# Hyperbolic loops of a graph kernel: two row blocks at once in halves of TensorE, the 65th coordinate apart, a degree-3 polynomial, tiles of 2x512

## The chip, the cores and the metric

The kernel runs on one core of a Trainium2 chip. The metric is the time of one execution on the device, in microseconds (us). An engine is named as the profile names it: PE is TensorE (PEld its weight loads), ACT is ScalarE, DVE is VectorE, POOL is GpSimd, SP is SyncE.

## The reference

Four graph layers follow each other on 3327 nodes of 64 features. Each takes `h = relu(layernorm(x))` and adds its result to `x`. Layers 0 and 3 are hyperbolic and are what is changed here; layers 1 and 2 (a decayed sum over neighbours, and a signed attention with two GRU cells) stay as they are. A hyperbolic layer, with c = 1 for layer 0 and c = 1/r^2 for layer 3:

```python
x_tan = _logmap0(x, C)
left = x_tan @ att_W[:D] + att_b
right = x_tan @ att_W[D:]
adj_att = jax.nn.sigmoid(left + right.T) * adj
x_local = _logmap(x[:, None, :], x[None, :, :], C)
support_t = jnp.einsum('ij,ijd->id', adj_att, x_local)
return _proj(_expmap(x, support_t, C), C)
```

`_logmap` of a pair of nodes needs their scalar product and their squared lengths, then an artanh. So for every pair of the 3327 x 3327 there is a product of two vectors, a function of it, a sigmoid and a mask, and the results are summed over neighbours with the vectors as weights. `adj` holds zeros and ones; about 0.5% are ones.

## The kernel before

The nodes are padded to 3328 = 26 blocks of 128 (T = 26, P = 128, NP = 3328, D = 64). `adj` comes in transposed, so that the neighbours lie on the partitions. The program first runs `hyperbolic_series` (layer 0, `adj` read from memory), `plain_decay` (which also builds masks of 8 bits), `plain_gat`, and `hyperbolic_series` again (layer 3, with the masks), and stores the result. Each part also writes whether its shortcuts held for all nodes; if one did not, a second, general path computes everything anew. In `hyperbolic_series` that test is `x2 >= X2_MIN`, the squared length of every real node.

`hyperbolic_series` has three stages.

1. Preparation. `norm_relu` makes H (node on the partition). `rows` holds per node 65 numbers: 64 coordinates 2*h/(x2-1) and as the 65th (x2+1)/(x2-1). `to_columns` (L114, L115: transposes on PE, copies on ACT) turns `rows` into LT, 65 x 3328; RT is LT with the first 64 rows negated, so that a product of LT and RT over 65 rows gives the argument of the polynomial for a pair. The tangent vectors `xt` are transposed too (`xtT`). `pl` (L333) multiplies them with the left half of the weights, spread over 128 columns, which makes `leftB`, the left term on every partition; `pr` (L337) makes `right`, one column per block.
2. The loop. It goes over four column chunks of 832 nodes and in each over 13 pairs of row blocks. For a pair: the mask (13 DMAs per chunk in the first call, masks in the second; `drop_diagonal`, L146, clears the diagonal), two sigmoids on ACT (L357), one product with the mask on POOL (L359). Then for each of the two row blocks: two matmuls of 416 columns into L (L364), two Square passes on ACT that make a polynomial of degree 4 (L368, L369), two combined operations on DVE (L370, L372), which give the weights w, and two matmuls that add `rows` x w into `acc` (L375), 65 x 416 each. L has three buffers, y and w two, `acc` one. All data of these matmuls are f32.
3. The end. `acc` is copied (L379), turned back by `to_rows` (L124), scaled (L389), and `move` does the remaining steps on DVE for all nodes at once.

The program is written with a framework that sets the waits and orders each engine's instructions by a planned order of its own; on PE, products of later blocks stand ahead of sums of earlier ones.

In `plain_decay` and `plain_gat`, matmuls with 64 weight columns stand in pairs that write the two halves of the partitions of one accumulator (L909, L974), with 16-bit weights and 16- or 8-bit data:

```python
for o in range(2):
    PE.matmul(acc[h][o * D:(o + 1) * D, :], parts[k][:, b, :], w[:, o, h, :],
              start=first and k == 0, stop=last and k == 2)
```

Of the kernel before, what the change touches and what calls it, by code (L numbers as in the profile page):

```python
# [9 lines left out]
F32 = mybir.dt.float32  # L10
# [8 lines left out]
P = 128  # L19
# [9 lines left out]
G0, G1, G2, G3, G4 = 0.30970640316, -0.36098355479, 0.46940675477, -1.28660460234, 2.86920527402  # L29
X2_MIN = 18.0  # L30
# [3 lines left out]
def tile_gnn4(ctx: ExitStack, tc: tile.TileContext, x, adjT, att0, b0, w1, bias1, w_gat, a_gat,  # L34
# [26 lines left out]
    g1_c = column(G1 - 0.5, "g1_c")  # L61
    g2_c = column(G2, "g2_c")
# [8 lines left out]
    def wide(t, n=D):  # L71

        return t[:, :, None].to_broadcast([P, T, n])
# [161 lines left out]
    def hyperbolic_series(att, b_att, r, min_norm, min_norm2, ok, masks=None):  # L235
# [8 lines left out]
        W = 2 * BK  # L244
        R = D + 1
        with ExitStack() as st:
            pers = st.enter_context(tc.tile_pool(name="hs", bufs=1))
            rows = pers.tile([P, T, R], F32, name="rows")
# [3 lines left out]
            LT = pers.tile([R, NP], F32, name="LT")  # L252
            RT = pers.tile([R, NP], F32, name="RT")
            leftB = pers.tile([P, NP], F32, name="leftB")
            right = pers.tile([P, T], F32, name="right")
            maxn2 = pers.tile([P, 1], F32, name="maxn2")
# [3 lines left out]
            with tc.tile_pool(name="hsp", bufs=1) as tp, tc.tile_pool(name="hsps", bufs=2, space=PSUM) as ps:  # L260
                w_l = tp.tile([D, 1], F32, name="w_l")
                w_r = tp.tile([D, 1], F32, name="w_r")
                nc.sync.dma_start(w_l, att[:D])
                nc.sync.dma_start(w_r, att[D:])
                bcol = tp.tile([P, 1], F32, name="bcol")
                nc.scalar.dma_start(bcol, bcast_rows(b_att))
                w_lb = tp.tile([D, P], F32, name="w_lb")
                V.tensor_copy(w_lb, w_l.to_broadcast([D, P]))
# [30 lines left out]
                V.tensor_mul(rows[:, :, :D], hs, wide(ia))  # L299
                V.tensor_scalar(rows[:, :, :D], rows[:, :, :D], 2.0, None, op0=OP.mult)  # L300
                V.scalar_tensor_tensor(rows[:, :, D], x2, 1.0, ia, op0=OP.add, op1=OP.mult)
# [19 lines left out]
                xt = tp.tile([P, T, D], F32, name="ln_sq")  # L321
                V.tensor_mul(xt, H, wide(z))

                to_columns(ps, LT, rows, R)
                sgn = tp.tile([R, 1], F32, name="sgn")
                V.memset(sgn, 1.0)
                V.memset(sgn[:D], -1.0)
                V.tensor_scalar(RT, LT, sgn, None, op0=OP.mult)
                xtT = tp.tile([D, NP], F32, name="xtT")
                to_columns(ps, xtT, xt, D)  # L330
                for k in range(NP // BK):
                    pl = ps.tile([P, BK], F32, name="pl")
                    PE.matmul(pl, w_lb, xtT[:, k * BK:(k + 1) * BK], start=True, stop=True)  # L333
                    V.tensor_copy(leftB[:, k * BK:(k + 1) * BK], pl)
                pr = ps.tile([P, T], F32, name="pr")
                for t in range(T):
                    PE.matmul(pr[:, t:t + 1], xtT[:, t * P:(t + 1) * P], w_r, start=True, stop=True)  # L337
                V.tensor_scalar(right, pr, bcol, None, op0=OP.add)  # L338

            with tc.tile_pool(name="hsw", bufs=2) as wk, tc.tile_pool(name="hsps", bufs=3, space=PSUM) as ps, \  # L340
                    tc.tile_pool(name="hsacc", bufs=1, space=PSUM) as pa:
                for c in range(NP // W):
                    c0 = c * W
                    acc = [pa.tile([R, BK], F32, name=f"acc{h}") for h in range(2)]
                    for b2 in range(T // 2):
                        if masks is None:
                            adj = wk.tile([P, 2, W], F32, name="adj", bufs=4)
                            nc.sync.dma_start(adj, adjT[2 * b2 * P:(2 * b2 + 2) * P, c0:c0 + W]
                                              .rearrange("(s p) i -> p s i", p=P))
                            for s in range(2):  # L350
                                drop_diagonal(adj[:, s, :], 2 * b2 + s, c0, W)
                        else:
                            adj = masks[b2][:, :, c0:c0 + W]
                        sig = wk.tile([P, 2, W], F32, name="sig")
                        for s in range(2):
                            b = 2 * b2 + s
                            A.activation(sig[:, s, :], leftB[:, c0:c0 + W], AF.Sigmoid,  # L357
                                         bias=right[:, b:b + 1])
                        G.tensor_tensor(sig, adj, sig, op=OP.mult)  # L359
                        for s in range(2):  # L360
                            b = 2 * b2 + s
                            L = ps.tile([P, 2, 512], F32, name="L")
                            for h in range(2):
                                PE.matmul(L[:, h, :BK], LT[:, b * P:(b + 1) * P],  # L364
                                          RT[:, c0 + h * BK:c0 + (h + 1) * BK], start=True, stop=True)
                            Lu = L[:, :, :BK]
                            y = wk.tile([P, 2, BK], F32, name="y")
                            A.activation(y, Lu, AF.Square, scale=0.5, bias=g1_c)  # L368
                            A.activation(y, y, AF.Square, bias=g2_c)  # L369
                            V.scalar_tensor_tensor(Lu, Lu, 0.5 * G3, y, op0=OP.mult, op1=OP.add)  # L370
# [729 lines left out]
```

## Time and profile before

| what | value |
|---|---|
| time, median of 3 runs (lowest, highest) | 1271.29 us (1270.71, 1277.21) |
| the profiled execution: its own time, its span | 1277.46 us, 1275.7 us |
| mean granted TensorE clock in it | 0.895 |
| busy: PE, DVE, ACT, POOL | 997.5, 823.7, 726.2, 393.6 us |
| loop of the first hyperbolic call, start to its last sums | 57.7 to 395.2 us |
| loop of the second hyperbolic call | 889.6 to 1216.5 us |

The profile is one execution, and the times in it are counted from the start of its span. A group of instructions is one line of the kernel on one engine with one kind of operands: its count, its busy time, the mean length of one, then the idle time of the engine just before them and what ended most of it. A record of a matmul is longer than the spacing of matmuls, because they are pipelined: what one costs in a row of many is read from the distance of their starts, and in the timeline from a merged group (its length less that of the last record, divided by the count less one). The first words of a group's operands give weights and output partitions: 128*64 is 128 rows by 64 columns of weights.

### The profile page before, as it was taken

The page shows a single profiled execution, that of the slowest core. Times are in us where ns is not written, and L with a number is a line of the kernel's source. Part 1 is how long each engine was busy: PE and PEld are TensorE (multiplying, and loading weights), DVE is VectorE, ACT ScalarE, POOL GpSimd, SP SyncE. Part 2 cuts the span into 40 slices and gives each one's busy share as a digit, 9 for nine tenths or more (in the row PEclk, how much of TensorE's full clock was granted, in tenths as well). Part 3 has the DMA queues.
Part 4 walks back from the last instruction along what each step waited for, and adds up shares of the span by engine and source line. Part 5 has one row for each costly group of instructions (what it writes and reads, how often), then busy time and mean ns, then how long its engine had stood idle before and what let it go on. Part 6 is the DMA issues. An engine that isn't in the chain of part 4 may idle for free.

```text
span 1275.7 us, 11381 instructions
## 1 busy us (share of the span) xinstructions
PE 997.5 (78%) x4051; PEld 477.7 (37%) x4051; DVE 823.7 (65%) x937; ACT 726.2 (57%) x851; POOL 393.6 (31%) x166
## 2 busy tenths in 40 slices
PE   0989999999993037888996699919899998999910
PEld 0634444344441032333332476406344443444400
DVE  7255666566668969994933402793466676667787
ACT  1378879889883013444453001413689999899910
POOL 0065665665661000201210000000445555455500
PEclk9789989999997568999999799966799999999965
DMA  2153444444420009992910000000000000000001
GB/s 28 57 171 121 134 134 134 134 136 135 139 101 0 0 21 341 302 305 82 297 47 9 6 2 1 1 0 1 0 1 1 0 1 1 0 1 1 0 3 28
DMA packets 41844, 91.62 MB, mean 72 GB/s; under 512 B 15152, under 2 KB 15152, under 8 KB 41776
## 3 DMA queue, kind: packets, MB, share of 16 engines
q1 hardware_dynamic: 37200, 90.76, 21.9%
q10 hardware_dynamic: 4576, 0.02, 0.3%
q8 instruction: 34, 0.56, 0.2%
q14 instruction: 34, 0.28, 0.1%
HBM read 89.92 MB, written 0.85 MB: 71 GB/s over the span
## 4 chain that ended last, share of the span: by engine, by line
PE 45%; DVE 22%; ACT 17%; POOL 7%; issue 6%; DMA 2%; ACTq 0%; DVEq 0%; POOLq 0%; SPq 0%
PE acc L375 13%; PE L L364 9%; POOL sig L359 7%; PE acc L909 6%; ACT y L369 5%; DVE w L372 5%; PE acc L974 4%; ACT w L902 4%; PE cnt L904 4%; ACT sig L357 3%; ACT y L368 3%; DVE L L370 3%; PE cnt L900 2%; PE pt L114 2%; DVE prod L153 1%
## 5 line engine op out<-in xcount | busy, mean ns | idle before, releaser
L375 PE MATMUL acc<-w,rows 128*65 128x416 f32 x832 | 341.3, 535 | 39.9 <-DVE w L372 38.1
L364 PE MATMUL L<-RT,LT 65*128 65x416 f32 x832 | 334.2, 527 | 0.7 <-DVE right L338 0.7
L370 DVE SCALAR_TENSOR_TENSOR L<-L,y 128x832 f32<-128x832 f32 x208 | 213.8, 1030 | 185.4 <-ACT y L369 181.7
L359 POOL TENSOR_TENSOR sig<-mask,sig 128x1664 f32<-128x1664 fp8e4 x52 | 164.6, 3167 | 385.2 <-ACT sig L357 375.1
L372 DVE SCALAR_TENSOR_TENSOR w<-L,sig 128x832 f32<-128x832 f32 x208 | 212.5, 1024 | 52.9 <-POOL sig L359 35.8
L368 ACT ACTIVATE y<-L,g_c 128x832 f32<-128x832 f32 x208 | 195.8, 943 | 76.5 <-PE L L364 76.5
L359 POOL TENSOR_TENSOR sig<-adj,sig 128x1664 f32<-128x1664 f32 x52 | 193.1, 3716 | 102.2 <-ACT sig L357 102.1
L364 PEld LDWEIGHTS L<-RT,LT 65*128 65x128 f32 x832 | 162.6, 196 | 149.9 <-issue 146.9
L369 ACT ACTIVATE y<-y,g_c 128x832 f32<-128x832 f32 x208 | 203.9, 983 | 3.5
L357 ACT ACTIVATE sig<-leftB,right 128x832 f32<-128x832 f32 x208 | 201.2, 977 | 7.5 <-DVE w L372 7.4
L375 PEld LDWEIGHTS acc<-w,rows 128*65 128x65 f32 x832 | 108.9, 141 | 242.7 <-DVE w L372 117.1
L902 ACT ACTIVATE w<-cnt,ebias 128x832 bf16<-128x832 f32 x104 | 93.7, 950 | 110.9 <-PE cnt L900 68.8
L146 POOL TENSOR_TENSOR mask<-mask,offdiag 128x128 fp8e4<-128x128 fp8e4 x26 | 23.4, 902 | 248.0 <-PE cnt L904 241.6
L895 DVE SCALAR_TENSOR_TENSOR same<-adj 128x1664 bf16<-128x1664 f32 x52 | 99.0, 1904 | 0.0
L909 PE MATMUL acc<-w,sup 128*64 128x416 bf16 x624 | 94.0, 349 | 0.0
L904 PE MATMUL cnt<-mask,rest 128*128 128x416 fp8e4 x208 | 54.1, 341 | 28.7 <-ACT w L902 28.7
L900 PE MATMUL cnt<-mask,after 128*128 128x416 fp8e4 x208 | 55.2, 350 | 9.7 <-DVE mask L892 9.7
L974 PE MATMUL acc<-mask,h 128*64 128x416 fp8e4 x624 | 60.9, 345 | 0.7 <-ACT hP L827 0.7
L909 PEld LDWEIGHTS <-sup 128*64 128x64 bf16 x624 | 38.1, 110 | 49.9 <-issue 37.0
L892 DVE TENSOR_SCALAR mask<-adj 128x1664 fp8e4<-128x1664 f32 x52 | 54.9, 1056 | 1.1 <-DMA adj<-in 1.1
L114 PE MATMUL pt<-ident,rows 128*65 128x128 f32 x52 | 12.0, 426 | 54.4 <-DVE zs L86 30.2
L114 PE MATMUL pt<-ident,H 128*64 128x128 f32 x26 | 5.3, 366 | 61.4 <-DVE H L106 61.4
(247 smaller groups left out, 657.9 us busy)
## 6 DMA issues: line engine op xcount, KB each, us to landing
adj<-in SPq DMA_DIRECT2D x104, 832.0 KB, 4.8
X<-in SPq DMA_DIRECT2D x1, 832.0 KB, 7.8
out<-X SPq DMA_DIRECT2D x1, 832.0 KB, 6.0
gw<-in SPq DMA_DIRECT2D x8, 48.0 KB, 2.3
gb<-in ACTq DMA_DIRECT2D x8, 0.8 KB, 2.0
w_l<-in SPq DMA_DIRECT2D x2, 0.2 KB, 5.2
bcol<-in ACTq DMA_DIRECT2D x2, 0.5 KB, 5.4
w_r<-in SPq DMA_DIRECT2D x2, 0.2 KB, 4.1
```

The source lines that it names most:

```text
L357: A.activation(sig[:, s, :], leftB[:, c0:c0 + W], AF.Sigmoid, bias=right[:, b:b + 1])
L359: G.tensor_tensor(sig, adj, sig, op=OP.mult)
L364: PE.matmul(L[:, h, :BK], LT[:, b * P:(b + 1) * P], RT[:, c0 + h * BK:c0 + (h + 1) * BK], start=True, stop=True)
L368: A.activation(y, Lu, AF.Square, scale=0.5, bias=g1_c)
L369: A.activation(y, y, AF.Square, bias=g2_c)
L370: V.scalar_tensor_tensor(Lu, Lu, 0.5 * G3, y, op0=OP.mult, op1=OP.add)
L372: V.scalar_tensor_tensor(w, Lu, G4 - 0.5 * G3, sig[:, s, :].rearrange("p (h i) -> p h i", h=2), op0=OP.add, op1=OP.mult)
L375: PE.matmul(acc[h], rows[:, b, :], w[:, h, :], start=(b == 0), stop=(b == T - 1))
L902: A.activation(w[:, o, :, :], cnt[o][:, :, :BK], AF.Exp, scale=-LN2, bias=ebias)
L904: PE.matmul(cnt[o][:, h, :BK], rest, mask[:, o, h * BK:(h + 1) * BK], start=False, stop=True, skip_group_check=True)
L909: PE.matmul(acc[h][o * D:(o + 1) * D, :], parts[k][:, b, :], w[:, o, h, :], start=first and k == 0, stop=last and k == 2)
L974: PE.matmul((acc[k] if i < 3 else cnt[k])[o * D:(o + 1) * D, :], w, mask[:, o * HP + k * BK:o * HP + (k + 1) * BK], start=b == 0 and i in ...
```

## The change

The loops of both hyperbolic calls get another form, and what they need is prepared and finished otherwise.

- *Products.* The 64 coordinates are laid out twice, on partitions 0 to 63 and 64 to 127 (XT). The products of two row blocks use rows 0 to 63 and 64 to 127 of the array (L415). The 65th coordinate is split into three 16-bit parts; its product, with a constant added, is a matmul of 9 rows in 16 bits per row block, on rows 0 to 31 and 32 to 63 (E and F, transposed into ET and FT; L419).
- *Polynomial.* Degree 3 instead of 4: one Square on ACT per tile instead of two (L422), a combined operation and a product on DVE (L423, L425). The threshold X2_MIN goes from 18 to 22.
- *Tiles.* One tile holds both row blocks by 512 columns; there are seven column chunks, six of 512 and one of 256. y, L and w are handled once per pair of row blocks.
- *Sums.* The sums of the two row blocks go into the two halves of one accumulator (L428), and those of the 65th coordinate into one of four groups of 32 columns of a second one (L433; `rows0` holds the coordinate and 31 zeros). At the end of a chunk both are copied by ACT (L438) and folded and transposed by matmuls with `halves` and `one_c` (L444, L445) into M.
- *Left and right.* They are made by DVE (a product and a sum over the features each) instead of by matmuls; `left` is put as three 16-bit parts into F and spread over the partitions at the start of each chunk by a matmul with `pick` (L394).

All line numbers in this section are those of the changed kernel. The diff, cut to its core:

```diff
-G0, G1, G2, G3, G4 = 0.30970640316, -0.36098355479, 0.46940675477, -1.28660460234, 2.86920527402
-X2_MIN = 18.0
+G0, G1, G2, G3 = -0.3851200397, -1.4315723663, 0.0289761757, 1.8129648238
+X2_MIN = 22.0
...
-        W = 2 * BK
-        R = D + 1
+        W = 512
+        NF = 12
...
+                for t0 in range(0, T, 4):
+                    n = min(4, T - t0)
+                    pt = ps.tile([P, 4 * P], F32, name="pt")
+                    for k in range(n):
+                        PE.transpose(pt[:D, k * P:(k + 1) * P], rows[:, t0 + k, :], ident)
+                        PE.matmul(pt[D:, k * P:(k + 1) * P], rows[:, t0 + k, :], ident, start=True, stop=True)
+                    A.activation(XT[:, t0 * P:(t0 + n) * P], pt[:, :n * P], AF.Copy)
...
-                xt = tp.tile([P, T, D], F32, name="ln_sq")
-                V.tensor_mul(xt, H, wide(z))
-
-                to_columns(ps, LT, rows, R)
...
-                to_columns(ps, xtT, xt, D)
-                for k in range(NP // BK):
-                    pl = ps.tile([P, BK], F32, name="pl")
-                    PE.matmul(pl, w_lb, xtT[:, k * BK:(k + 1) * BK], start=True, stop=True)
-                    V.tensor_copy(leftB[:, k * BK:(k + 1) * BK], pl)
-                pr = ps.tile([P, T], F32, name="pr")
-                for t in range(T):
-                    PE.matmul(pr[:, t:t + 1], xtT[:, t * P:(t + 1) * P], w_r, start=True, stop=True)
+                for k, o in ((0, left), (1, right)):
+                    sq = tp.tile([P, T, D], F32, name="ln_sq")
+                    V.tensor_mul(sq, H, wlr[:, k, None, :].to_broadcast([P, T, D]))
+                    V.reduce_sum(o, sq, axis=AX.X)
+                    V.tensor_mul(o, o, z)
...
+                pl = parts3(left, "pl")
+                V.tensor_copy(F[:, :, 9:12], pl)
+                for dst, src in ((ET, E), (FT, F)):
+                    to_columns(ps, dst, src, D)
...
+                    PE.matmul(Ll[:, 0, :n], pick, FT[:NF, cs], start=True, stop=True)
+                    leftB = wk.tile([P, W], F32, name="leftB", bufs=2)
+                    V.tensor_copy(leftB[:, :n], Ll[:, 0, :n])
...
-                            for h in range(2):
-                                PE.matmul(L[:, h, :BK], LT[:, b * P:(b + 1) * P],
-                                          RT[:, c0 + h * BK:c0 + (h + 1) * BK], start=True, stop=True)
...
-                            A.activation(y, Lu, AF.Square, scale=0.5, bias=g1_c)
-                            A.activation(y, y, AF.Square, bias=g2_c)
-                            V.scalar_tensor_tensor(Lu, Lu, 0.5 * G3, y, op0=OP.mult, op1=OP.add)
...
-                            for h in range(2):
-                                PE.matmul(acc[h], rows[:, b, :], w[:, h, :],
-                                          start=(b == 0), stop=(b == T - 1))
+                        for s in range(2):
+                            q, e = slice(s * D, (s + 1) * D), slice(s * 32, s * 32 + 9)
+                            b = slice((2 * b2 + s) * P, (2 * b2 + s + 1) * P)
+                            PE.matmul(L[:, s, :], XT[q, b], XT[q, cs], start=True, stop=False)
+                        for s in range(2):
+                            q, e = slice(s * D, (s + 1) * D), slice(s * 32, s * 32 + 9)
+                            b = slice((2 * b2 + s) * P, (2 * b2 + s + 1) * P)
+                            PE.matmul(L[:, s, :], ET[e, b], FT[e, cs], start=False, stop=True)
+
+                        y = wk.tile([P, 2, W], F32, name="y", bufs=2)[:, :, :n]
+                        A.activation(y, L, AF.Square, scale=-0.5, bias=shift_c)
+                        V.scalar_tensor_tensor(L, y, G3, L, op0=OP.add, op1=OP.mult)
+                        w = wk.tile([P, 2, W], F32, name="w")[:, :, :n]
+                        V.tensor_mul(w, L, sig)
                         for s in range(2):
                             b = 2 * b2 + s
+                            PE.matmul(accs[0][s * D:(s + 1) * D, :n], rows[:, b, :], w[:, s, :],
+                                      start=b2 == 0, stop=b2 == T // 2 - 1)
...
+                            g = b % 4 * 32
+                            PE.matmul(accs[1][g:g + 32, :n], rows0[:, b, :], w[:, s, :],
+                                      start=b < 4, stop=b >= T - 4)
...
+                    for k in range(nt):
+                        PE.matmul(Lm[:, k, :D], sums[0][:, k * P:(k + 1) * P], halves, start=True, stop=True)
+                        PE.matmul(Lm[:, k, D:], sums[1][:, k * P:(k + 1) * P], one_c, start=True, stop=True)
+                    V.tensor_copy(M[:, t0:t0 + nt, :], Lm)
...
-                to_rows(ps, RT, R, lambda t0, n, src: V.tensor_copy(M[:, t0:t0 + n, :], src))
```

## The prediction

> **What bounds the kernel now.** I read the page first (busy shares, slices, the chain that ended last, groups), then the busy time in the two stretches where the changed loops run, then the timeline for starts. From the page:
>
> ```profile
> PE 997.5 (78%) x4051; PEld 477.7 (37%) x4051; DVE 823.7 (65%) x937; ACT 726.2 (57%) x851; POOL 393.6 (31%) x166
> PE 45%; DVE 22%; ACT 17%; POOL 7%; issue 6%; DMA 2%; ACTq 0%; DVEq 0%; POOLq 0%; SPq 0%
> L375 PE MATMUL acc<-w,rows 128*65 128x416 f32 x832 | 341.3, 535 | 39.9 <-DVE w L372 38.1
> L364 PE MATMUL L<-RT,LT 65*128 65x416 f32 x832 | 334.2, 527 | 0.7 <-DVE right L338 0.7
> L370 DVE SCALAR_TENSOR_TENSOR L<-L,y 128x832 f32<-128x832 f32 x208 | 213.8, 1030 | 185.4 <-ACT y L369 181.7
> L368 ACT ACTIVATE y<-L,g_c 128x832 f32<-128x832 f32 x208 | 195.8, 943 | 76.5 <-PE L L364 76.5
> L357 ACT ACTIVATE sig<-leftB,right 128x832 f32<-128x832 f32 x208 | 201.2, 977 | 7.5 <-DVE w L372 7.4
> ```
>
> TensorE leads the chain, and L364 and L375 have 832 records each where the program issues 416 calls: an f32 matmul is two records, each with a weight load of its own. The two loops, first call and second (columns: stretch, length, busy time of PE, PEld, DVE, ACT, POOL, then the granted clock):
>
> ```profile
> 57.70:395.20 337.50, 314.51 (x833) 136.51 (x834) 210.91 (x208) 285.39 (x320) 204.40 (x80) 0.96 0.41 132
> 889.60:1216.50 326.90, 310.02 (x833) 135.31 (x834) 212.26 (x208) 284.65 (x320) 164.62 (x52) 0.96 0.00 1
> ```
>
> PE is busy 93 to 95%, ACT 85%: so the price of a matmul sets these 664.4 us. The timeline gives prices by starts (start, length of the group):
>
> ```profile
> 1100.38 1.56 PE L364 MATMUL L<-RT,LT 65*128 65x416 f32 x4
> ...
> 730.54 2.29 PE L974 MATMUL acc<-mask,h 128*64 128x416 fp8e4 x24
> ...
> 541.80 0.52 PE L904 MATMUL cnt<-mask,rest 128*128 128x416 fp8e4 x2
> 542.25 1.24 PE L909 MATMUL acc<-w,sup 128*64 128x416 bf16 x10
> 543.42 0.35 PE L900 MATMUL cnt<-mask,after 128*128 128x416 fp8e4 x1
> ...
> 38.30 0.96 PE L333 MATMUL pl<-xtT,w_lb 64*128 64x416 f32 x2
> ...
> 43.36 0.94 PE L337 MATMUL pr<-w_r,xtT 64*128 64x1 f32 x8
> ```
>
> - f32: (1.56 - 0.51 of the last record) / 3 = 0.35 us per record of 416 columns. A loop has 832: 291 us, of 337.5 and 326.9. The rest is some 10 us of halved clock and the waits.
> - Halves of columns do overlap in 16 and 8 bits: L974 alternates between the halves and needs (2.29 - 0.34) / 23 = 0.085 us per record, half of a full-width record (two of L904: 0.52 - 0.34 = 0.18).
> - Going from full width to halves costs: L904's last stream ends at 541.80 + 2 x 0.175 = 542.15, L909 starts at 542.25; back again its last pair ends near 542.25 + 1.24 - 0.34 + 0.175 = 543.33 and L900 starts at 543.42. Some 0.095 us each way.
> - After a switch the weight load is exposed too: L333, first after transposes in another form, starts its second record 0.96 - 0.51 = 0.45 us after the first, 0.10 over the usual 0.35.
> - A matmul of one column with 128 f32 weights (L337) costs (0.94 - 0.25) / 7 = 0.10 us, 0.11 without the first start, which overlaps.
>
> **The change, part by part.** The unit is now a pair of row blocks by 512 columns: 6 x 13 = 78 full pairs and 13 half-wide ones per loop. In units of such area the old loop paid 337.5/84.5 = 3.99 and 326.9/84.5 = 3.87 us.
>
> *Other engines.* By slopes between 416 (0.60, 0.65 us) and 832 columns, ACT pays 2 x 0.69 + 1.12 = 2.5 us a pair (before 2.90 x 1024/832 = 3.6; the second Square is gone), DVE 1.21 + 1.20 = 2.4 as before, POOL 3.72 x 1024/1664 = 2.3. All lie under PE, so the shorter polynomial and the wider tile buy only fewer waits.
>
> *TensorE.* One f32 record of 512 columns streams 0.35 x 512/416 = 0.43 us, one bf16 record 0.175 x 512/416 = 0.215. A pair needs X (two products of 64 rows, f32), E (two of 9 rows, bf16), A (two sums into 64 columns, f32), C (two sums into 32 columns, f32); every one is in another form of the array than its neighbour, so a pair has four switches: 0.095 each plus the exposed load, X 0.20, E 0.11, A 0.145, C 0.12, together 0.575.
>
> How far X, A and C overlap is the open cost; no row shows an f32 matmul in halves, or halves of rows in any type. Each issues first block high, first block low, second block high, second block low. The low record needs the half that the high one is streaming into. In all stretches that I read matmuls start in the program's order: none overtakes an earlier one. So the second block can't start with the first block's high record, only with its low one: three slots instead of four (L974 alternates at every record, and so gets two at once). I take that, since it follows from L974's overlap and the order of starts alike; the ends are two slots (as L974) and four (no overlap). With three: X 1.29 + 0.20, E 0.215 + 0.11, A 1.29 + 0.145, C 1.29 + 0.12 = 4.66 us; half-wide 2.62. Per loop 78 x 4.66 + 13 x 2.62 = 397.5.
>
> The order in which the program issues TensorE's work adds to it: of 182 X pairs 48, or 24 per loop, are split by A and C of another pair, each at one slot and one switch more: 24 x 0.63 = 15. New are the closing sums (L444, L445: 26 blocks x 4 records x 0.11 = 11.5) and the spreading of `left` (7 x 0.33 = 2.3, switches 1.4). Sum 428; halved clock 10 as before; at each of seven column ends PE waits for the copies of the sums, some 0.7 (a 512-wide ACT copy) + 0.3: 7. So 445 per loop. The next chunk's chain (left copied, sigmoid, mask, w: about 6 us) hides behind three pairs of X and E and the closing sums, 3 x 1.8 + 2 us; without that cover 3 us per chunk. Over both loops 2 x 445 - 664.4 = +226.
>
> A rule speaks against the change twice. The Trainium skill, "TensorEngine Tiling (Array Packing)", Key Properties, says that a change of tiling mode, not of tile, drains the engine; the rows above agree at 0.095 us. The Trainium skill, "TensorE: Matmul & The Clock Gate", Part 3, says that matmuls are strictly first in, first out in start and end, while its span model has packed tiles 4 ns apart; by the first the sum is that above, by the second alone each f32 pair would take two slots, the rival below.
>
> *Before and after the loops.* Gone are `pl` (8 matmuls), `pr` (26) and the transposes of `xt`:
>
> ```profile
> 46.90 2.98 PE pl L333 x4
> 49.88 7.49 PE pr L337 x36
> ```
>
> In come 52 transposes for E and F, of which F's 26 wait for the last of `left`: 52 records of 0.11 to 0.21 us (full or halved clock), about what `pr` cost. DVE gains two products and two reductions (7.5 us) and some 30 small operations (3 to 6), loses 4.9; PE loses pl's 16 records (6 to 11). Net -4 a call, then -1.5 for the row transposes at the end: -11 in all, between -25 and +5. `leftB` by chunk puts a copy before the first sigmoid (+1, in that).
>
> Sum against the profiled execution (1277.46 us, span 1275.7): 1277.5 + 226 - 11 = 1492; the median of the runs lies 6 lower: **1486 us**.
>
> **The rivals.**
> - *Full overlap, switches as measured.* If the second block starts with the first: X 1.06, E 0.325, A 1.005, C 0.98 = 3.37 a pair; the loop 263 + 26 (half-wide) + 24 x 1.06 for the split ones + 15 + 17 = 346: 1277.5 + 27 - 11 - 6 = 1288, up to 1340 if PE still waits for w as it does now. The four switches eat what the halves save. For it: L974's pairs. Against: the order of starts.
> - *Full overlap and free switches: faster.* If the next form's weights load while the last one streams, each pair saves 0.575 more, 57 per loop: 1288 - 114 = 1174. It needs both; the sign turns when the switches of a pair cost under about 0.47 us. Against: the 0.095 and 0.10 us above; for: those rows are from other types and forms, and a switch between two forms of halves is not among them.
> - *Columns overlap, rows don't* (no row shows the latter): X +0.43, E +0.215: +44 per loop, 1574.
> - *No overlap in f32 at all:* 6.16 a pair, loop 562: 1720.
> - That the second path runs (nodes under the new threshold 22): worked out from the reference's inputs, the smallest is 23.5, so no.
>
> **How the numbers follow.** Three slots 0.50; columns only 0.08; no overlap 0.05; full overlap at measured switches 0.17 (0.04 of it within half a per cent, about what a measurement of this kernel can tell from no change); full overlap with cheap switches 0.20. Slower 0.50 + 0.08 + 0.05 + 0.13 = 0.76, same 0.04, faster 0.20. The range reaches to the columns-only case with its error, 1600, leaving out the last, and down to 1225, leaving out about half of the fast case (1174 to 1265). The likeliest case's own range is 1430 to 1530 (exposed loads 0.3 to 0.8 a pair).
>
> **What would show it.** In the profile after: starts of L415 and L428 in an X or A group at 0, 0.43, 0.43, 0.86 us (three slots) against 0, 0, 0.43, 0.43; a gap of 0.1 us or more at each change among L415, L419, L428, L433; PE busy over 95% in the loops with ACT and DVE under 60%; loops of 430 to 460 us. Wrong if the second block's first record starts with the first block's, if starts after a switch come without a gap, or if a loop's rest is idle time before PE.

## The result, and the profile after

The changed kernel takes **1369.22 us** (median of 4 runs, 1366.99 to 1372.89). The kernel before, on the same chip, takes 1272.87 us. The ratio is 1.0755, 95% interval 1.0716 to 1.0794. It is slower, as forecast, by 96 us where 215 was forecast (1486 less the 1271.29 of before); the time lies between the rival "full overlap, switches as measured" (1288, up to 1340) and the forecast of 1486.

The page's lines that answer to those of before (line, engine, operands, count; busy time, mean length; idle time before, and what ended it):

```profile
PE 1068.5 (78%) x5125; PEld 374.1 (27%) x5125; DVE 835.9 (61%) x961; ACT 584.9 (43%) x799; POOL 416.6 (30%) x254
...
PE 22%; DVE 9%; ACT 3%; issue 1%; DVEq 0%; ACTq 0%
...
L423 DVE SCALAR_TENSOR_TENSOR L<-y,L 128x1024 f32<-128x1024 f32 (+1 forms) x182 | 209.7, 1152 | 220.7 <-ACT y L422 220.7
...
L415 PE MATMUL L<-XT 64*128 64x512 f32 (+1 forms) x728 | 258.0, 648 | 0.0
...
L428 PE MATMUL acc<-w,rows 128*64 128x512 f32 (+1 forms) x728 | 190.3, 602 | 52.6 <-DVE w L425 52.6
...
L433 PE MATMUL acc<-w,rows 128*32 128x512 f32 (+1 forms) x728 | 184.4, 586 | 0.0
```

ACT has fallen from 726 to 585 us and DVE has stayed, as forecast; PE has grown, and the sums L428 wait 52.6 us for w. The chain that ended last accounts for only 35% of this span, so its shares are not compared with those of before. The busy time in the two loops of the changed kernel (stretch, length, busy PE, PEld, DVE, ACT, POOL, granted clock):

```profile
67.27:432.20 364.93, 337.53 (x1379) 88.16 (x1378) 215.87 (x195) 210.70 (x288) 210.66 (x117) 0.97 0.42 122
939.06:1309.40 370.34, 345.15 (x1379) 89.06 (x1378) 215.97 (x195) 210.88 (x288) 171.43 (x91) 0.95 0.00 1
```

The loops hold 735.3 us in place of 664.4: +71. The first starts at 67.3 instead of 57.7 us, 506.9 us lie between them instead of 494.4, and the tail is 1.6 us shorter: +20.5 outside the loops, where -11 was forecast.

The timeline of PE in the first loop shows what a pair costs (start, length of the group, form, records):

```profile
201.35 1.13 PE L415 MATMUL L<-XT 64*128 64x512 f32 x4
202.41 1.08 PE L428 MATMUL acc<-w,rows 128*64 128x512 f32 x4
203.42 1.05 PE L433 MATMUL acc<-w,rows 128*32 128x512 f32 x4
204.40 0.39 PE L419 MATMUL L<-FT,ET 9*128 9x512 bf16 x2
205.28 1.08 PE L428 MATMUL acc<-w,rows 128*64 128x512 f32 x4 [0.49 <-DVE w L425]
206.29 1.05 PE L433 MATMUL acc<-w,rows 128*32 128x512 f32 x4
207.27 1.13 PE L415 MATMUL L<-XT 64*128 64x512 f32 x4
208.34 0.39 PE L419 MATMUL L<-FT,ET 9*128 9x512 bf16 x2
208.65 1.13 PE L415 MATMUL L<-XT 64*128 64x512 f32 x4
```

Four records of X, A or C occupy two slots, not three: A starts 202.41 - 201.35 = 1.06 us after X, C 1.01 after A, E 0.98 after C, and X 0.31 after E. That sums to 3.36 us a pair; the rival said 3.37, the forecast 4.66. In the trace's records the first two X start at 201.349 and 201.355, the next two at 201.882 and 201.888. Two pairs repeat every 7.30 us (201.35 to 208.65): 6.73 of work, and 0.56 that the sums wait for w.

Not all products have this rhythm. In each loop 48 groups of X hold the two records of one product alone, with other work before and behind them (start, length of the group, form, records):

```profile
181.53 1.12 PE L415 MATMUL L<-XT 64*128 64x512 f32 x2
182.58 0.39 PE L419 MATMUL L<-FT,ET 9*128 9x512 bf16 x2
182.90 1.13 PE L415 MATMUL L<-XT 64*128 64x512 f32 x4
183.96 0.39 PE L419 MATMUL L<-FT,ET 9*128 9x512 bf16 x2
```

Such a group takes 182.58 - 181.53 = 1.05 us, as long as four records of two blocks (183.96 - 182.90 = 1.06). Against 24 groups of four with the same records, 48 groups of two cost some 25 us more per loop.

### The profile page after: what moved, and what is told of

It is laid out like the page before. It is cut to its first block, busy times and chain, and to the rows that moved or that the text cites. A ratio compares the mean times of both kernels' runs of the same rounds, so it can differ in the third digit from the quotient of the medians.

```text
span 1367.1 us, 13434 instructions
## 1 busy us (share of the span) xinstructions
PE 1068.5 (78%) x5125; PEld 374.1 (27%) x5125; DVE 835.9 (61%) x961; ACT 584.9 (43%) x799; POOL 416.6 (30%) x254
## 5 line engine op out<-in xcount | busy, mean ns | idle before, releaser
L423 DVE SCALAR_TENSOR_TENSOR L<-y,L 128x1024 f32<-128x1024 f32 (+1 forms) x182 | 209.7, 1152 | 220.7 <-ACT y L422 220.7
L422 ACT ACTIVATE y<-L,shift_c 128x1024 f32<-128x1024 f32 (+1 forms) x182 | 190.9, 1049 | 179.3 <-PE L L419 179.3
L408 ACT ACTIVATE sig<-leftB,right 128x512 f32<-128x512 f32 (+1 forms) x364 | 233.7, 682 | 77.6 <-DVE w L425 67.9
L415 PE MATMUL L<-XT 64*128 64x512 f32 (+1 forms) x728 | 258.0, 648 | 0.0
L410 POOL TENSOR_TENSOR sig<-mask,sig 128x1024 f32<-128x1024 fp8e4 (+1 forms) x91 | 171.4, 1887 | 250.6 <-ACT sig L408 202.3
L410 POOL TENSOR_TENSOR sig<-adj,sig 128x1024 f32<-128x1024 f32 (+1 forms) x91 | 199.7, 2202 | 139.9 <-ACT sig L408 111.9
L428 PE MATMUL acc<-w,rows 128*64 128x512 f32 (+1 forms) x728 | 190.3, 602 | 52.6 <-DVE w L425 52.6
L425 DVE TENSOR_TENSOR w<-L,sig 128x1024 f32<-128x1024 f32 (+1 forms) x182 | 209.1, 1149 | 21.5 <-POOL sig L410 2.0
L433 PE MATMUL acc<-w,rows 128*32 128x512 f32 (+1 forms) x728 | 184.4, 586 | 0.0
L415 PEld LDWEIGHTS L<-XT 64*128 64x128 f32 x728 | 71.8, 194 | 102.4 <-issue 95.8
L428 PEld LDWEIGHTS acc<-w,rows 128*64 128x64 f32 x728 | 36.5, 137 | 157.8 <-DVE w L425 130.8
L419 PE MATMUL L<-FT,ET 9*128 9x512 bf16 (+1 forms) x364 | 70.3, 383 | 0.0
L343 PE MATMUL pt<-ident,rows 128*64 128x128 f32 x52 | 21.9, 421 | 59.6 <-DVE rows L336 31.1
L433 PEld LDWEIGHTS acc<-w,rows 128*32 128x32 f32 x728 | 26.5, 109 | 141.0 <-issue 141.0
```

The source lines that it names most:

```text
L408: A.activation(sig[:, s, :], leftB[:, :n], AF.Sigmoid, bias=right[:, 2 * b2 + s:2 * b2 + s + 1])
L415: PE.matmul(L[:, s, :], XT[q, b], XT[q, cs], start=True, stop=False)
L419: PE.matmul(L[:, s, :], ET[e, b], FT[e, cs], start=False, stop=True)
L422: A.activation(y, L, AF.Square, scale=-0.5, bias=shift_c)
L423: V.scalar_tensor_tensor(L, y, G3, L, op0=OP.add, op1=OP.mult)
L425: V.tensor_mul(w, L, sig)
```

## The experiments

Theory: the halves overlap in full, switches of form cost what the prediction read, and the rest of the loss is the waits for w, the preparation and the clock. Rivals: the loss is partial overlap; the loss is the switches alone; the loss belongs to the polynomial or the wide tile. Beside each run stood runs of the kernel before on the same chip (medians 1271.7 to 1274.5 us), and the ratios are to these. How long the clock was halved is read from the clock records of the trace; the granted clock in the rows is their mean.

**Both products in the same half.**

```diff
-PE.matmul(L[:, s, :], XT[q, b], XT[q, cs], start=True, stop=False)
+PE.matmul(L[:, s, :], XT[:D, b], XT[:D, cs], start=True, stop=False)
```

> The changed kernel, but both products of a pair use rows 0 to 63 of the array (the result stays the same, since both halves hold the same data). Theory (the two halves really run at once: in the trace after, records of the two halves start 0.007 us apart and the next two 0.43 to 0.53 later): the products then take four streams of 0.43 us instead of two, +0.86 us a full pair, of which the 0.29 us that PE now waits per pair for w may absorb a part; over 2 x 84.5 pairs +96 to +145 us, so 1465 to 1515 us. Rival (three streams, as predicted before: only one of the four records overlaps): +0.43 us less the wait, +24 to +73 us. Rival (starts are shown together, but the streams share one path): no change, 1369.

Measured: 1549.71 us, ratio 1.2186 (1.2142 to 1.2230); loops 457 and 454. From PE's timeline in this kernel:

```profile
219.71 1.98 PE L415 MATMUL L<-XT 64*128 64x512 f32 x4
221.62 0.39 PE L419 MATMUL L<-FT,ET 9*128 9x512 bf16 x2
221.94 1.98 PE L415 MATMUL L<-XT 64*128 64x512 f32 x4
```

The four X now take 221.62 - 219.71 = 1.91 us, four streams of 0.43 and the switch, where they took 1.06. So two blocks overlap because they lie in different halves, and all of the overlap is there in the changed kernel. The total is 35 us over the upper bound; in this run the clock is halved for 143 and 138 us of the loops (20.5 and 37.5 in the changed kernel), which was not in the estimate.

**Two of the four switches taken away**: E in 64 rows (the same form as X), C in 64 columns (the same form as A).

```diff
-rows0 = pers.tile([P, T, 32], F32, name="rows0")
+rows0 = pers.tile([P, T, D], F32, name="rows0")
...
-PE.matmul(L[:, s, :], ET[e, b], FT[e, cs], start=False, stop=True)
+PE.matmul(L[:, s, :], ET[q, b], FT[q, cs], start=False, stop=True)
...
-PE.matmul(accs[1][g:g + 32, :n], rows0[:, b, :], w[:, s, :], ...)
+PE.matmul(accs[1][s * D:(s + 1) * D, :n], rows0[:, b, :], w[:, s, :], ...)
```

> The changed kernel, with two of the four switches of form of a pair taken away and nothing else: E has 64 rows (zeros below the 9) like X, C has 64 columns (one full, 63 zeros) like A. Theory (each of these two switches costs the 0.10 us that the trace after shows between forms, and the cycle E, y, L, w, A, C, X, E sets a period of 7.3 us for two pairs, in which two of the switches lie): -0.1 us a pair, 1345 to 1360 us. Rival (PE's work alone decides): -0.2 us a pair, 1325 to 1340. Rival (what stands between forms is not the change of form but the load of other weights): no change, 1369.

Measured: 1354.92 us, ratio 1.0642 (1.0587 to 1.0698); loops 357.4 and 359.9. A and C (now L432) in PE's timeline of this kernel:

```profile
204.64 1.08 PE L428 MATMUL acc<-w,rows 128*64 128x512 f32 x4
205.55 1.03 PE L432 MATMUL acc<-w,rows 128*64 128x512 f32 x4
```

and its line among the waits (who waits for whom: us in total, times, the longest):

```profile
PE acc L428 <- DVE w L425: 71.8, 71, 4.3
```

From A to C it is now 0.91 us instead of 1.01: the last A record's stream goes from 0.52 to 0.42 us before the next form begins. A switch costs PE 0.10 us, as read from the kernel before. But the wait for w grew from 52.6 to 71.8 us, and two switches gave 14 us in all. Of the 7.5 and 10.4 us by which the loops fell, some 7 in the second are less halved clock (23.9 us in place of 37.5). That the loop was limited in part by the chain E, y, L, w, which fewer switches don't shorten, is argued from the longer wait.

**XT by one transpose of doubled rows.**

```diff
-for k in range(n):
-    PE.transpose(pt[:D, k * P:(k + 1) * P], rows[:, t0 + k, :], ident)
-    PE.matmul(pt[D:, k * P:(k + 1) * P], rows[:, t0 + k, :], ident, start=True, stop=True)
-A.activation(XT[:, t0 * P:(t0 + n) * P], pt[:, :n * P], AF.Copy)
...
+V.tensor_copy(rows2, rows[:, :, None, :].to_broadcast([P, T, 2, D]))
+to_columns(ps, XT, rows2.rearrange("p t k d -> p t (k d)"), P)
```

> The changed kernel, but the twofold transposed coordinates XT come from one transpose of 128 columns per block (the rows laid out twice by a DVE copy) instead of a transpose for the lower and an f32 matmul with the identity for the upper half. Theory (the change of form between the two costs: 0.97 us per block, 25 us per call in the trace after, and ACT's copies of XT hold back the logarithms that left and right wait for): 26 transposes at 0.11 to 0.21 us, so the loops start some 15 us earlier in each call, 1369 becomes 1330 to 1345. Rival (DVE's chain to left and right sets the start): under 8 us in all.

Measured: 1339.46 us, ratio 1.0540 (1.0498 to 1.0582); the first loop starts at 49.8, its length is 368.3, the second's 369.5. First PE's timeline in the changed kernel:

```profile
31.07 0.39 PE L343 MATMUL pt<-ident,rows 128*64 128x128 f32 x1 [31.07 <-DVE rows L336]
31.40 0.69 PE L344 MATMUL pt<-ident,rows 128*64 128x128 f32 x2
32.02 0.42 PE L343 MATMUL pt<-ident,rows 128*64 128x128 f32 x1
```

and in this one:

```profile
33.09 5.82 PE L117 MATMUL pt<-ident,rows 128*128 128x128 f32 x26 [33.09 <-DVE p L300]
```

A transpose (L343) and an f32 identity matmul (L344, two records) alternate, 0.95 to 0.97 us per block, 25 us for 26 blocks; the plain transposes take 5.8. Both run slowly: their transposes start some 0.21 us apart in a row, those from 59 us on 0.11. The former are 78 records, which would take some 17 us at the rate of the latter; so most of the 25 us is their number, and the rest comes with the alternation. PE ends the former at 56.3 us; ACT's copies of XT end then too, and its logarithms for `left` come behind them, at 58.1, so that F and the loop start late. With the doubled rows everything outside the loops is 14 us shorter than before (7.9 earlier, 4.7 less between, 1.1 at the end): the forecast's -11. The preparation costs the change 30 us of its 96.

**The polynomial of degree 3 alone**, in the kernel before.

```diff
...
-A.activation(y, Lu, AF.Square, scale=0.5, bias=g1_c)
-A.activation(y, y, AF.Square, bias=g2_c)
-V.scalar_tensor_tensor(Lu, Lu, 0.5 * G3, y, op0=OP.mult, op1=OP.add)
+A.activation(y, Lu, AF.Square, scale=-0.5, bias=shift_c)
+V.scalar_tensor_tensor(Lu, y, G3, Lu, op0=OP.add, op1=OP.mult)
```

> The kernel before, with the polynomial of degree 3 alone (a 66th row carries its constant): tiles, matmuls, preparation and end as before. Theory (PE's streams, 291 us of a loop, and its waits at chunk starts decide; ACT's second Square lies beside them): 1255 to 1275 us. Rival (ACT, busy 85% of the loops before, causes the waits for w): loops of 300 to 312 us, 1220 to 1240 us.

Measured: 1287.6 us, ratio 1.0121 (1.0063 to 1.0180); loops 344.7 and 329.0. A miss: less work on ACT made it 1.2% slower. Among its waits (us in total, times, the longest):

```profile
PE acc L374 <- DVE w L372: 56.7, 104, 3.2
```

The wait of the sums for w rose from 38.1 to 56.7 us. The framework plans the order anew with the shorter chain, and products and sums now come in longer bursts: in the first loop 25 groups of products have ten records, where most have four in the kernel before. That the order is the cause is argued from that and not shown by a run.

**Degree 3 and tiles of 2x512, products and sums on the whole array** (66 rows, 65 columns).

```diff
...
+PE.matmul(L[:, s, :], LT[:, b], RT[:, cs], start=True, stop=True)
-PE.matmul(L[:, s, :], XT[q, b], XT[q, cs], start=True, stop=False)
-PE.matmul(L[:, s, :], ET[e, b], FT[e, cs], start=False, stop=True)
...
+PE.matmul(acc[:, :n], rows[:, b, :D + 1], w[:, s, :], start=b == 0, stop=b == T - 1)
-PE.matmul(accs[0][s * D:(s + 1) * D, :n], rows[:, b, :], w[:, s, :], ...)
-PE.matmul(accs[1][g:g + 32, :n], rows0[:, b, :], w[:, s, :], ...)
```

> The polynomial of degree 3 and tiles of 2x512 stay, but products and sums use the whole array again: products over 66 rows (64 coordinates, the 65th, and a constant), sums into 65 columns. Theory (the halves do not pay because of the switches: X+E 1.37 and A+C 1.99 us a pair in the trace after, against 8 records of 0.43 = 3.44 us without any switch; the shorter polynomial and wider tile are the part that helps, since PE waits less): loops of 305 to 325 us, preparation near that of the kernel before, 1225 to 1265 us, faster than before. Rival (halves help as such, and the loss comes from the tile size or from DVE and ACT working on longer tiles): 1369 or more. Rival (PE work alone counts): loops 3.44/3.37 times those of after, 1375.

Measured: 1264.96 us (ten runs, 1250.54 to 1271.77), ratio 0.9913 (0.9872 to 0.9953); loops 328.6 and 331.7, longer than the 305 to 325 expected, so that the time lies at the upper end of its range. Neither the polynomial nor the tile is what costs 96 us; the step from here to the halves costs 104.

**Halves in one place alone**: products in halves with whole sums, and whole products with sums in halves.

```diff
 # products in halves, sums whole
+PE.matmul(acc[:, :n], rows[:, b, :], w[:, s, :], start=b == 0, stop=b == T - 1)
 # products whole, sums in halves
+PE.matmul(L[:, s, :], LT[:, b], RT[:, cs], start=True, stop=True)
```

> The changed kernel, but the sums use the whole array (65 columns into one accumulator, no second one for the 65th coordinate); the products stay in halves. Theory (A and C in halves with their two switches cost 1.99 us a pair, four whole records 1.72 and one switch of about 0.15): -0.12 us a pair, -20 us in all, and the closing sums get cheaper, 8 us per loop: 1330 to 1350. Rival (in the loops the wait for w decides and not PE's work): 1355 to 1370.

Measured: 1384.67 us, ratio 1.0887 (1.0846 to 1.0929); loops 373.5 and 373.3. A miss: 15 us slower than the changed kernel instead of faster. Waits for w are 61.4 us in place of 52.6, and the clock is halved for 48 us in each loop.

> The changed kernel with whole-array products over 66 rows (no E); the sums stay in halves with the 65th coordinate apart. Theory (prices add up: 1.72 for the products, 0.20 + 1.01 + 0.98 for the rest, 3.9 us a pair): loops of 345 to 370 us, preparation 18 us a call shorter than in the changed kernel, 1315 to 1340 us. Rival (the two parts act independently of each other, so that what the sums in halves cost, -15 by the run with whole sums, is a gain here): 1250.

Measured: 1403.86 us, spread over 1373.7 to 1419.5, no ratio. A miss too: in the profiled run the clock is halved for 85 and 98 us of the loops; at half speed that is worth some 45 us each, and without it the loops would be some 355, inside what was expected. Even the lowest of its runs, 1373.7, lies over the 1340 expected. These two runs, and the first, raised the question of the clock.

**The whole-array form with the seams cleared**: `left` spread ahead of the loops, the sums turned behind them, two accumulators, two buffers in place of three for `sig` and w.

```diff
-acc = pa.tile([D + 1, W], F32, name="acc", bufs=1)
-leftB = wk.tile([P, W], F32, name="leftB", bufs=2)
+acc = pa.tile([D + 1, W], F32, name="acc", bufs=2)
...
-PE.transpose(Lm[:, k, :], sums[:, k * P:(k + 1) * P], ident[:D + 1, :D + 1])
+A.activation(ST[:, cs], acc[:, :n], AF.Copy)
+# behind the loop:
+to_rows(ps, ST, D + 1, lambda t0, n, src: V.tensor_copy(M[:, t0:t0 + n, :], src))
```

> The kernel with whole-array products and sums, degree 3 and 2x512 tiles, with three changes to what surrounds the matmuls: left is spread over the partitions for all chunks before the loop, the sums are only copied in the loop and turned after it (two accumulators), and mask, weights and sigmoid have two buffers instead of three, with which the planned order on PE becomes an even alternation of two products and two sums. Theory (of its loops of 329 and 332 us 290 are streams, the rest waits for w, mostly at the seven chunk starts and ends): loops of 298 to 312 us, in all 1200 to 1235 us. Rival (PE's streams and exposed weight loads fill the loop): 1250 to 1265 us.

Measured: **1214.83 us**, ratio 0.9545 (0.9494 to 0.9596). The busy time in its first loop (columns as above):

```profile
55.20:358.60 303.40, 299.46 (x727) 119.26 (x728) 208.40 (x182) 203.75 (x277) 210.70 (x117) 0.98 0.50 145
```

and the rhythm of products and sums in PE's timeline there:

```profile
200.19 1.88 PE L388 MATMUL L<-RT,LT 66*128 66x512 f32 x4
201.91 1.88 PE L396 MATMUL acc<-w,rows 128*65 128x512 f32 x4
203.63 1.88 PE L388 MATMUL L<-RT,LT 66*128 66x512 f32 x4
```

PE is busy 99%, and a pair takes 203.63 - 200.19 = 3.44 us: eight records of 0.43, no switch. Against 3.36 in halves this is the balance of the change's TensorE work: the halves save 3.44 - 2.79 = 0.65 us of streams, E included, and the four switches give 0.57 back. It holds for pairs whose products stand together, not for the groups of two records above.

**The same in halves, by `left` alone** (with the doubled transpose; `sig` and w have two buffers in place of three, while y and L keep theirs, other than the expectation says).

```diff
-PE.matmul(Ll[:, 0, :n], pick, FT[:NF, cs], start=True, stop=True)
-leftB = wk.tile([P, W], F32, name="leftB", bufs=2)
...
+for c0 in range(0, NP, W):          # ahead of the loop
...
+    PE.matmul(pb[:, :cs.stop - c0], pick, FT[:NF, cs], start=True, stop=True)
+    V.tensor_copy(leftB[:, cs], pb[:, :cs.stop - c0])
```

> The changed kernel's halves with the two edits around the loops alone: the points transposed doubled in one step per block, and the row `left` spread ahead of the loops. The loop's own steps and their order are left as in the changed kernel, only its buffers of y, L and w are 2 in place of 3. Theory (the loop is bound by PE's 3.37 us a pair and its waits for w, and neither edit touches these): 1300 to 1340, loops 350 to 368. Rival (the gain of the whole-array kernel with `left` spread ahead, 50 us, came from the spreading itself and not from the order of L and sums, so it shows here too): 1270 to 1300.

Measured: 1378.46 us, ratio 1.0812 (1.0771 to 1.0852); loops 395.6 and 385.1. Both expectations missed; it is 39 us slower than with the doubled transpose alone. The seam between two tiles of 512 columns, in PE's timeline:

```profile
100.47 1.05 PE L431 MATMUL acc<-w,rows 128*32 128x512 f32 x4
103.81 1.16 PE L426 MATMUL acc<-w,rows 128*64 128x512 f32 x4 [2.29 <-DVE w L423]
104.90 1.92 PE L431 MATMUL acc<-w,rows 128*32 128x512 f32 x4
106.75 0.69 PE L442 MATMUL L<-halves,sum 128*128 128x64 f32 x2
```

PE waits 2.29 us for the tile's last w, and its order has no other work ahead of these sums; then the same four C records take 1.92 in place of 1.05 us: the clock is halved, from 104.7 us on, for 17.1 us, and so at each of the first loop's next four seams. The busy time in that loop (columns as above, the granted clock 0.87):

```profile
52.11:447.70 395.59, 368.64 (x1370) 99.01 (x1370) 211.87 (x188) 208.54 (x285) 211.18 (x117) 0.87 0.38 111
```

Altogether it is halved for 99 and 77 us of the two loops, where the kernel with the doubled transpose alone had 31 and 34; half of that difference is 56 us, more than the 43 by which the loops grew.

**The seam moved.** The last pair's sums come behind the next tile's first products, the turning of the sums behind its fourth pair. The edit puts every pair's sums behind the next pair's products, so that the planned order changes inside a tile too:

```diff
+if late is not None:
+    add(*late)                      # the pair before, across tiles
+    if b2 == 0:
+        pending = take(c0 - W, W)   # copies of the sums
+if b2 == 4 and pending is not None:
+    turn(*pending)                  # L442, L443 of above
+    pending = None
...
+late = (n, b2, w)
```

> The kernel with the two edits around the loops (label e_halves_ahead), and in it only the seam between two tiles of 512 columns moved: the sums of a tile's last pair come behind the first products of the next tile, and the turning of the sums behind its fourth pair. In e_halves_ahead PE waits 2.3 us for the tile's last w with nothing else queued, and each of these five pauses is followed by 17.1 us of halved clock (99 and 77 us of it in the two loops). Theory (the pause at the seam brings the halved clock): without the pause at most 35 us of halved clock in a loop, and loops of 345 to 365, in all 1290 to 1330. Rival (the halved clock comes of the work in halves, wherever it pauses): 75 to 100 us of halved clock in each loop as before, loops 375 to 395, in all 1345 to 1380.

Measured: **1274.17 us**, ratio 1.0004 (0.9979 to 1.0028); loops 333.1 and 332.8. A seam in PE's timeline of this kernel:

```profile
118.98 1.08 PE L405 MATMUL acc<-w,rows 128*64 128x512 f32 x4 [0.49 <-DVE w L460]
119.99 1.05 PE L410 MATMUL acc<-w,rows 128*32 128x512 f32 x4
120.97 0.43 PE L397 MATMUL L<-halves,sum 128*128 128x64 f32 x2
```

and the busy time in its two loops:

```profile
52.39:385.50 333.11, 316.85 (x1369) 82.61 (x1370) 211.16 (x188) 206.46 (x285) 211.39 (x117) 0.99 0.45 132
882.68:1215.44 332.76, 316.49 (x1370) 82.57 (x1370) 211.15 (x188) 206.32 (x284) 171.55 (x91) 0.99 0.00 1
```

The clock is halved for 9 us in each loop, the granted clock is 0.99, and 104 us are gone: the theory's side, and 16 us below its range. The count closes: 99.0 - 9.3 and 76.9 - 8.5 us of halved clock cost half of that, 45 and 34 us; the loops fell by 62.5 and 52.3. The rest, 18 us each, answers to two things that the traces count, together some 20: in the first loop PE waits 16.3 us for w in place of 26.8, and 24 X groups have two records in place of 42 (0.53 us each). So the halved clock came with the pauses, or with the order around them, and not with the halves as such.

**Two pairs at a time**: X for two pairs, E for two, A for two, C for two, so that four switches serve two pairs; with the two edits around the loops, and w in four buffers.

```diff
+Ls = products(pairs)       # X of both pairs, then E of both
+if late is not None:
+    add(*late)             # A of both pairs before, then C of both
+late = (pairs, [weights(L, sig) for L, sig in zip(Ls, sigs)])
```

> The changed kernel's halves, with the points transposed doubled in one step per block and the row `left` spread ahead of the loops, and the loop's steps taken for two pairs of blocks at a time: four products X, four products E, four sums A, four sums C in a row, so that four switches of form serve two pairs, and the four column groups of C stand side by side. Theory (halves overlap in full; a switch of form costs what it cost in the trace of the change): two pairs need X 4 x 0.43 + 0.20 = 1.92 us, E 0.52, A 1.72 + 0.145 = 1.87, C 0.86 + 0.12 = 0.98, together 5.3 us in place of 6.73, which takes 0.72 us x 91 pairs = 65 us from each loop of the run with the doubled transpose (368); loops 270 to 310, in all 1130 to 1220. Rival (the loop goes by the chain from E over y, L and w to the sums, and a batch of two makes that chain longer, since only three buffers of L are there): the waits for w grow by what the switches give, loops 340 to 380, in all 1285 to 1365.

Measured: 1271.81 us, ratio 1.0006 (0.9990 to 1.0021); loops 332.5 and 330.9, between theory and rival. PE waits 38 us for w in the first loop, 32.4 of it ahead of X, for a buffer of L; the clock is halved for 75 and 67 us. With the seam moved as above:

> The kernel that takes its steps for two pairs at a time (label e_batch, loops of 332 and 331 us with 75 and 67 us of halved clock and 38 us of waits for w in the first), with the same move of the seam between two tiles. Theory (what kept e_batch above its estimate were the pauses of 1.6 to 3.6 us around the seams and the halved clock behind them): at most 35 us of halved clock in a loop, loops 280 to 305, in all 1165 to 1220. Rival (it is the chain over y, L and w with three buffers of L that sets the time inside the tiles too): loops 315 to 332, in all 1235 to 1270.

Measured: **1209.71 us**, ratio 0.9504 (0.9465 to 0.9543), the lowest of all that ran. The rhythm in PE's timeline of this kernel:

```profile
125.15 1.13 PE L450 MATMUL L<-XT 64*128 64x512 f32 x4
127.02 1.13 PE L450 MATMUL L<-XT 64*128 64x512 f32 x4 [0.74 <-DVE w L463]
128.08 0.60 PE L455 MATMUL L<-FT,ET 9*128 9x512 bf16 x4
128.62 1.94 PE L407 MATMUL acc<-w,rows 128*64 128x512 f32 x8
130.48 1.06 PE L413 MATMUL acc<-w,rows 128*32 128x512 f32 x8
```

and the busy time in its two loops:

```profile
53.17:353.81 300.64, 268.43 (x1370) 78.69 (x1370) 200.43 (x188) 204.81 (x285) 209.65 (x117) 0.97 0.51 146
846.71:1148.05 301.34, 273.72 (x1369) 79.40 (x1370) 200.47 (x188) 204.97 (x285) 170.18 (x91) 0.95 0.00 1
```

Eight records of C in four column groups take the time of four in two (1.06 us), A and E of two pairs pay one switch each. PE is busy only 268 and 274 us of 301: the theory's total (1165 to 1220) came, but the rival's wait stays, 48.9 us ahead of L450 for a buffer of L in both loops. Against the whole-array kernel with its seams cleared (0.9494 to 0.9596) the intervals overlap.

## Why the prediction was right in sign and wrong in size

- **The failed step: "three slots instead of four".** The prediction took from the order of starts that "none overtakes an earlier one", so that the second block could join only at the first block's low record. The starts lie 6 or 7 ns apart, two and two (201.349, 201.355; 201.882, 201.888): two slots for X, A and C. The term was 4.66 us a pair and measured 3.36; over 78 full and 13 half-wide pairs, 110 us per loop too much. (The groups of two records, 24 split pairs in the prediction, were priced too low by the same step: 0.63 us more for each, where the trace shows 1.05.) The run with both products in one half shows that the half alone decides. The trace names neither the half nor the pass (high or low) of a record, so whether the low pass is overtaken or the passes are issued in another order than assumed stays open.
- **The sign was right without that step.** With two slots the prediction's own sum is its rival's 1288, 17 us over the kernel before. What made it 96 lies in terms outside the step, so the sign owes something to luck.
- On the rules weighed there: the starts agree with the packed tiles a few ns apart in the Trainium skill, "TensorE: Matmul & The Clock Gate", Part 3. Whether its rule of strict order in start and end holds here can't be read from rows that don't name the record; what was wrong was to make a slot of it.
- **Right: the price of a stream and of the switches.** 0.43 us a record, and 0.57 us for four switches (from 3.36 less 2.79 of streams); a switch removed was worth 0.10 us.
- **The rival's sum, with what it had too small.** "Full overlap, switches as measured" said loops of 346, with 7 in each for the column ends and 10 for the halved clock: measured 364.9 and 370.3, 43 us more in both. PE waits for w 27.4 and 25.2 us in the loops, 39 more than 14, as the rival's own condition allowed ("if PE still waits for w as it does now"). The clock is halved for 20.5 and 37.5 us, of which half is lost, 29 us, 9 more than 20. Together these are 48, against 43. Outside the loops -11 was +20.5: the prediction priced the transposes of E and F but not those of XT, which are in the diff; that is 32 us. 1288 + 43 + 32 = 1363, against 1369.
- **The halved clock does not set the two kernels apart.** By the same clock records it holds for 29.4 and 23.5 us of the loops of the kernel before, 52.9 us against 58.0. The prediction's 10 us a loop for its cost was 13 in that kernel.
- **Column ends at 7 us a loop were too cheap.** The prediction named the copies of the sums; what costs is that the last w of a tile has nothing to hide behind, and that a halved clock can follow. From the kernel with the doubled transpose to the one with the seam moved as well (and `left` ahead of the loops, and two buffers for `sig` and w), the loops fall from 368.3 and 369.5 to 333.1 and 332.8, and the time from 1339.46 to 1274.17.
- **Its test lines** worked as set: starts at 0, 0, 0.53, 0.53 us (0.43 and the exposed load of 0.10) ruled out three slots; PE busy 92.5 and 93.2% of the loops, not over 95%, pointed to waits; gaps at each change of form were there.

So of +96 us, 30 are the preparation. In the loops PE does work that it did not do there before: 25 us a loop for the X groups of two records, and 14 in the first loop for closing sums and `left`, near the 15 of the prediction; the waits for w are 52.6 us in place of 38.1. No run takes one of these terms away alone. With the preparation mended, `left` ahead and the seam moved, the kernel in halves stands level with the one before (1.0004), whose own seams are as they were. Against the whole-array kernel with its seams cleared (0.9545) it is some 59 us slower, its first loop 333.1 in place of 303.4 us. The traces of these two loops show where: 24 X groups of two records (13 us), waits for w of 16.3 us in place of 3.8, and 11 us of closing sums inside the loop. What the halves save in streams, the switches take, and the rest is lost beside them.

## What to carry to other kernels

Work out halves of the array per pair of products, streams saved against switches paid, and group equal forms over several tiles so that one switch serves many; pairs in turn (3.36 us) gain next to nothing over whole-array matmuls (3.44), and a product that stands without its partner takes as long as two (1.05 us). At the seam between tiles, put the next tile's first products ahead of the last sums: with the order inside the tiles that came with it, it was worth 104 us here, some 80 of them, half of the halved time, through the clock. And price every new transpose by form, not only the loop.

## What the runs showed of the hardware that was not expected

- A pause of 2.3 us on PE was followed by 17.1 us of halved clock, five times in one loop (granted clock 0.87 in it, 0.99 without the pauses). In the second loop the same pauses were followed by 6.8 to 17.1 us. The five halved stretches begin 61.4 us apart, 18 times 3.41, and the pauses 61.5, so that they may be one case that recurs. Lengths of halved stretches in the loops are multiples of 3.4 us. The Trainium skill, "TensorE: Matmul & The Clock Gate", Part 1, ties the halving to an idle window of some 3.4 us and the return to one busy window; here shorter pauses were enough, and the return took five. In the changed kernel pauses of some 1.25 us before a tile's last sums were mostly followed, some 5 to 8 us later, by 3.4 to 6.8 us, but not at the first two tile ends (120.5 and 174.9 us); in the first loop of the whole-array kernel with the seams as they were, pauses of 1.4 to 1.6 us at its six inner tile ends were followed by none. What sets onset and length is open.
- Four column groups of 32 with f32 data run side by side: eight records in the 1.06 us of four.
- Two forms in turn cost more than their records: 25 us for the 78 records of XT's preparation, where 26 in one form take 5.8 (78 would take some 17).
